# A graph layer's product copied by VectorE, and one eviction of the attention layer moved ahead of a norm in ScalarE's order

## The chip, the cores and the metric

The kernel runs on one core of one Trainium2 chip. A core has five engines with instruction streams of their own: TensorE (PE, with its weight loads shown apart as PEld), VectorE (DVE), ScalarE (ACT), GpSimd (POOL) and SyncE (SP), which in this kernel issues all DMA transfers. [...]The metric is the device time of the program in microseconds, lower is better: the median of several runs.

## The reference

The input is 64 images `x` of 256 rows by 512 columns in fp32, and one 256 x 256 graph `adj` that all of them share. Two layers follow each other, each with a residual and a layer norm over the columns:

```
mi = x @ Wi.T;  mj = x @ Wj.T
x  = layernorm(x + deg * (mi + b) + a @ mj)          # a = adj as float, deg = its row sums
q, k, v = x @ Wq.T + bq, x @ Wk.T + bk, x @ Wv.T + bv    # 8 heads of 64 columns
s  = where(adj == 0, -inf, q @ k.T / 8);  o = softmax(s) @ v
x  = layernorm(x + o @ Wo.T + bo)
```

Everything is computed in fp32. A matmul of fp32 operands appears as two PE instructions in the trace.

## The kernel before

**Tiling.** An image is held as two tiles of 128 rows. Images are worked on in pairs; pair g is `b1 = 2g` and `b2 = 2g + 1`. The main loop runs 31 times. Pass g holds the attention of pair g and, woven into it, layer 0 of pair g+1, and at its end the q, k and v products of pair g+1. One pass lasts about 96 us.

**Products in seven steps.** Products of a 2 x 2 block matrix with a 2 x 2 block weight are done by the scheme of Strassen and Winograd: seven products of blocks and some sums (`S1` to `S4` on the left, `T1` to `T4` on the right, the latter made once). Each step function issues one product on PE and then the instructions that take its bank of PSUM away. Several products share a bank: they are added up in it, and such a later product has to wait until the earlier content has been read. There are three banks of this kind (`ps_m`, tag `mm`).

**Layer 0** (`l0_steps`) has step1 to step7. Step4 (bank y) is read by VectorE (line 542). Step5 makes bank z from `S1` and `T1` and copies it to `mj[:, 1]` (line 547). Step6 adds into bank y and is read by VectorE as `u3` (line 551); POOL adds `u3` to `mj[:, 1]` (line 552), and `split` cuts the sum into two parts, `hi` on ScalarE (line 524) and `lo` on POOL (line 525). Step7 adds into bank z, and so needs step5's copy to be done; it is read at line 561. `neighbours` multiplies the graph by `hi` and `lo`. `take` forms the residual and the norm's statistics of a row tile, whose last part, `rstd`, is made on POOL (line 461). `give` applies the norm on ScalarE (lines 466 and 467: `shift`, then the row tile). `send_h` stores a row tile of the result in DRAM, and with the second tile starts a load that brings the image back in another layout as `hB` (line 603). VectorE transposes `hB` into `hT` (line 485), which feeds the q, k and v products. `sum_x` makes the four sums `xS` of the next image with lines 477 to 480 of VectorE.

**q, k, v and the output.** `qkv_steps` makes the seven steps of one of the three, `o_steps` those of the output product. `second_late` puts the third step ahead of the second. For q and k the first step is evicted by ScalarE with the bias (line 711, two instructions, `u`); the next one in the list adds into the same bank, and so needs that eviction to be done. Each step takes its weight block from a ring of nine buffers and starts the load of a later block into the buffer that became free (line 442).

**Attention.** `scores` multiplies q by k for two heads into a pair of banks (`ps`; two such pairs); VectorE adds the mask (line 805), ScalarE takes exponentials (line 809), POOL adds halves of them (`pk`, line 812). `values` multiplies by v, `divide` sums the denominators on PE (`den`), inverts them on VectorE (line 882) and spreads them by DMA. `neighbours` uses one of the score pairs too.

**Order.** The lists handed to `run` are written out by hand and set the order in which instructions are recorded. Instructions recorded through `in_order` keep that order on their engine; the framework's scheduler places the others by their operands. In the pass's tail the order is `o[0], neighbours, take1, take0, q[0], give1, send1, o[1], give0, send0, multiply`, the sums of the output product, then `k[0], q[1], k[1]`. On each engine instructions then run strictly in order.

Of the kernel before, what the change touches and what calls it, by code (L numbers as in the profile page):

```python
# [224 lines left out]
def unshifted_path(ctx, tc, flag, x, adj, wiT, wjT, b0, wqT, bq, wkT, bk, wvT, bv, woT, bo, out):  # L225
# [16 lines left out]
    nc = tc.nc  # L242
# [26 lines left out]
    def bank(name):  # L269
        return ps_m.tile([P, 512], F32, tag="mm", name=name)  # L270

    def score_banks(name):
        return ps_s.tile([P, 2, 512], F32, tag="sc", name=name)
# [8 lines left out]
    def in_order(ins):  # L282

        tc.keep_in_program_order(ins)
# [4 lines left out]
    def matmul(*args, **kw):  # L289
        in_order(nc.tensor.matmul(*args, **kw))  # L290
# [7 lines left out]
    def load_x(b):  # L298
        if b < B:
            xh[b] = p6.tile([P, NT, D], F32, tag="xh", name="xh")  # L300
            nc.sync.dma_start(out=xh[b], in_=x[b].rearrange("(t p) d -> p t d", p=P))
# [22 lines left out]
    xT, xS, hT, hS, qT, kT, vv, aoT, oS = ({} for _ in range(9))  # L324
# [48 lines left out]
    def add_bias(b):  # L373
        in_order(nc.gpsimd.tensor_tensor(xh[b], xh[b], degb, ALU.add))
# [76 lines left out]
    def norm_stats(t, order=anywhere):  # L451
        st = small.tile([P, 6], F32, tag="st", name="st")
        order(nc.vector.bn_stats(st, t))
        mv = small.tile([P, 2], F32, tag="mv", name="mv")
        nc.vector.bn_aggr(mv, st)
        ve = small.tile([P, 1], F32, tag="ve", name="ve")
        nc.vector.tensor_scalar(ve, mv[:, 1:2], EPS, None, ALU.add)
        below = small.tile([P, 1], F32, tag="below", name="below")
        order(nc.vector.tensor_scalar(below, mv[:, 0:1], -1.0, None, ALU.mult))  # L459
        rstd = small.tile([P, 1], F32, tag="rstd", name="rstd")  # L460
        nc.gpsimd.tensor_tensor(rstd, ve, mhalf, ALU.pow)  # L461
        return below, rstd

    def norm_apply(t, below, rstd, order=anywhere):
        shift = small.tile([P, 1], F32, tag="shift", name="shift")
        order(nc.scalar.activation(shift, below, AF.Identity, scale=rstd))  # L466
        order(nc.scalar.activation(t, t, AF.Identity, bias=shift, scale=rstd))  # L467
# [8 lines left out]
    def left_steps(f, order=anywhere):  # L476
        return [lambda: order(nc.vector.tensor_add(f["S1"], f["A21"], f["A22"])),
                lambda: order(nc.vector.tensor_sub(f["S2"], f["S1"], f["A11"])),
                lambda: order(nc.vector.tensor_sub(f["S3"], f["A11"], f["A21"])),
                lambda: order(nc.vector.tensor_sub(f["S4"], f["A12"], f["S2"]))]  # L480
# [21 lines left out]
    def l0_steps(b):  # L502
        banks, k = {}, {}

        def product(name, left, n, first):
            if first:
                banks[name] = bank("po")
            for c in range(2):
                matmul(banks[name], left[:, c, :], w0[:, n, c, :], start=(first and c == 0),
                                 stop=(c == 1), skip_group_check=True)  # L510

        def raw(t, h):
            return xT[b][:, 2 * h:2 * h + 2, t * P:(t + 1) * P]

        def keeper(name):
            k[name] = p3.tile([P, D], F32, tag="lu", name=name)
            return k[name]

        def add_scaled(t, src):
            nc.vector.scalar_tensor_tensor(xh[b][:, t, :], src, deg[:, t:t + 1], xh[b][:, t, :],  # L520
                                           ALU.mult, ALU.add)

        def split(t):
            nc.scalar.copy(k["hi"][:, t, :], k["mj"][:, t, :])
            nc.gpsimd.tensor_tensor(k["lo"][:, t, :], k["mj"][:, t, :], k["hi"][:, t, :].bitcast(F32),
                                    ALU.subtract)

        def step1():
            product("x", raw(0, 0), B11, True)
            nc.scalar.copy(keeper("u1"), banks["x"])  # L530

        def step2():
            product("w", raw(1, 1), T4, True)
            add_scaled(1, banks["w"])

        def step3():
            product("x", raw(0, 1), B21, False)
            add_scaled(0, banks["x"])

        def step4():  # L540
            product("y", xS[b]["S2"], T2, True)
            nc.vector.tensor_add(keeper("u2"), banks["y"], k["u1"])

        def step5():
            product("z", xS[b]["S1"], T1, True)
            k["mj"] = p1.tile([P, NT, D], F32, tag="mj", name="mj")
            nc.scalar.copy(k["mj"][:, 1, :], banks["z"])  # L547

        def step6():
            product("y", xS[b]["S3"], T3, False)  # L550
            nc.vector.tensor_add(keeper("u3"), banks["y"], k["u1"])
            nc.gpsimd.tensor_tensor(k["mj"][:, 1, :], k["mj"][:, 1, :], k["u3"], ALU.add)

            k["hi"] = p1.tile([P, NT, D], F32R, tag="hi", name="hi")
            k["lo"] = p1.tile([P, NT, D], F32R, tag="lo", name="lo")
            split(1)
            add_scaled(1, k["u3"])

        def step7():
            product("z", xS[b]["S4"], B22, False)  # L560
            nc.vector.tensor_add(k["mj"][:, 0, :], banks["z"], k["u2"])
            split(0)

        stats = {}

        def neighbours():
            k["pa"] = score_banks("pa")
            for i in (1, 0):
                for n, (j, part) in enumerate((j, part) for j in (1, 0) for part in ("hi", "lo")):
                    matmul(k["pa"][:, i, :], graph[:, j, i * P:(i + 1) * P], k[part][:, j, :],  # L570
                           start=(n == 0), stop=(n == 2 * NT - 1))

        def take(t):
            r = xh[b][:, t, :]
            in_order(nc.vector.tensor_add(r, k["pa"][:, t, :], r))
            stats[t] = norm_stats(r, in_order)

        def give(t):
            norm_apply(xh[b][:, t, :], *stats[t], in_order)


        return [step1, step2, step3, step4, step5, step6, step7, neighbours, lambda: take(1), lambda: take(0),
                lambda: give(1), lambda: send_h(b, 1), lambda: give(0), lambda: send_h(b, 0)]

# [83 lines left out]
    def second_late(steps):  # L668
        return [steps[0], steps[2], steps[1], *steps[3:]]
# [239 lines left out]
    def run(steps):  # L909
        for s in steps:  # L910
            s()
# [4 lines left out]
    def order_of(name):  # L916
        return [(name, n) for n in RIGHT]

    for g in range(-1, NG - 1):
        o, q, k, v = (order_of(name) for name in ("wo", "wq", "wk", "wv"))  # L920
# [18 lines left out]
    p, q = l0_steps(0), l0_steps(1)  # L939
# [18 lines left out]
    o = second_late(qk_steps(0, qT, "qT", bq_sb, bqd, True))  # L958
    k = second_late(qk_steps(0, kT, "kT", bk_sb, bkd, True))
# [22 lines left out]
    for g in range(NG - 1):  # L982
        load_x(NB * (g + 2))
        load_x(NB * (g + 2) + 1)
        work = layer0(g + 1)
        run(work[0])
        for w in range(2, NB * NC, 2):
            values(g, w - 2)
            values(g, w - 1)
            multiply()  # L990
            divide_two(g, w - 1)
            scores(g, w)()
            if w == 4:
                run(work[2])
            later = scores(g, w + 1)
            later()
            run(work[w // 2 if w < 4 else w // 2 + 1])
        w = NB * NC - 2
        values(g, w)
        values(g, w + 1)  # L1000
        multiply()
        o = o_steps(g)
        q = second_late(qk_steps(g + 1, qT, "qT", bq_sb, bqd))
        k = second_late(qk_steps(g + 1, kT, "kT", bk_sb, bkd, True))
        v = second_late(v_steps(g + 1, True))
        neighbours, take1, take0, give1, send1, give0, send0 = work[SLOTS + 1]
        divide_two(g, w + 1)
        run([o[0], neighbours, take1, take0, q[0], give1, send1, o[1], give0, send0, multiply,
             *left_steps(oS[g], in_order), k[0], q[1], k[1]])
        run(o[2:6] + work[SLOTS + 2] + [v[0], o[6], v[1]])  # L1010
        end = finish_steps(g)
        k = with_output_bias(g + 1, k)[2:]
        run(q[2:5] + end[:1] + q[5:6] + end[1:2] + q[6:7] + end[2:3] + k[:1] + end[3:4] + k[1:] + end[4:] + v[2:3])
        turn_x(NB * (g + 2))
        sum_x(NB * (g + 2))
        if g + 2 < NG:
            add_bias(NB * (g + 2))
        run(v[3:5])
        run([scores(g + 1, 0), scores(g + 1, 1)])
        run(v[5:])  # L1020
# [3 lines left out]
    g = NG - 1  # L1024
# [89 lines left out]
```

## Time and profile before

| | |
|---|---|
| time, median of 3 runs | 3117.08 us (3116.3 to 3118.02) |
| profiled execution, its own time | 3115.82 us |
| its span | 3113.4 us |
| granted TensorE clock | 0.999 |
| PE busy with matmuls | 3071.3 us, 99% |
| VectorE busy | 2148.5 us, 69% |
| POOL busy | 1520.8 us, 49% |
| ScalarE busy | 1007.8 us, 32% |
| DMA queue of SP | 48.3% of 16 engines' span |
| copy of `mj` on ScalarE (L547) | 64 times, 575 ns each |
| eviction of k's first step (L711, `u<-st,bk`) | 64 instructions, 458 ns each |

Times are those of one execution on the chip. A row of a timeline has the start in us from the span's start, the duration, the engine, the line, the operation, what is written and read, the shape, and in brackets how long the engine had been idle and what ended that. Rows of the same kind that follow each other are merged (x8: eight of them, with their common duration). A row of the waits has the waiting engine and line, what it waited for, the sum in us, the number of times and the longest one. A chain that ended last is given on the page too, but it covers nothing of the main loop here, so it is not used.

### The profile page before, as it was taken

To read this page: it belongs to the slowest core of one execution; us is meant where nothing else is said; L and a number is where in the kernel's file an instruction comes from. 1 tells how busy PE (TensorE), PEld (TensorE's weight loads), DVE (VectorE), ACT (ScalarE), POOL (GpSimd) and SP (SyncE) were. 2 spreads that over 40 slices of the span, in tenths; PEclk is the share of its full clock that TensorE was granted. 3 is DMA by queue.
4 is the path that set the end of the run, shared out by engine and by line. 5 is a ranking of instruction groups with operands and counts; after the bars stand their busy time and mean duration, and the time that the engine had idled before them with its cause. 6 is when DMAs were issued, how large, how long until landed. Compare 5 with 4: busy or idle time off the path is not lost. (4 is left out here: it accounts for less than half of the span.)

```text
span 3113.4 us, 42777 instructions
## 1 busy us (share of the span) xinstructions
PE 3071.3 (99%) x14598; PEld 2117.8 (68%) x14598; DVE 2148.5 (69%) x3234; ACT 1007.8 (32%) x1925; POOL 1520.8 (49%) x1255
## 2 busy tenths in 40 slices
PE   7999999999999999999999999999999999999998
PEld 5667766677766677666776667766677766677665
DVE  6776676766777667676667676667766667767665
ACT  2333333323333333333233332333333333323332
POOL 2544445544545445454454554454544546445453
PEclk9999999999999999999999999999999999999999
DMA  7345544455444555445553445544455444555333
GB/s 256 121 143 156 166 124 134 128 157 165 141 124 123 157 166 152 117 131 149 157 166 118 131 134 157 165 139 123 127 155 169 146 118 127 154 162 160 116 111 98
DMA packets 410395, 447.28 MB, mean 144 GB/s; under 512 B 40896, under 2 KB 300224, under 8 KB 409792
## 3 DMA queue, kind: packets, MB, share of 16 engines
q1 hardware_dynamic: 410176, 444.50, 48.3%
q8 instruction: 120, 1.97, 0.3%
q14 instruction: 99, 0.81, 0.1%
HBM read 340.79 MB, written 70.25 MB: 132 GB/s over the span
## 5 line engine op out<-in xcount | busy, mean ns | idle before, releaser
L461 POOL TENSOR_TENSOR rstd<-ve,mhalf 128x1 f32<-128x1 f32 x256 | 140.6, 554 | 724.3 <-DVE below L459 724.3
L812 POOL TENSOR_TENSOR pk<-pe 128x512 f32<-128x512 f32 x256 | 322.3, 1275 | 341.0 <-ACT pe L809 341.0
L290 PE MATMUL po<-w,xS 128*128 128x512 f32 x1024 | 470.4, 602 | 6.1 <-ACT mj L547 5.6
L290 PE MATMUL st<-hS,factor 128*128 128x256 f32 x2048 | 452.7, 379 | 1.2 <-DVE u L685 1.2
L290 PEld LDWEIGHTS st<-hS,factor 128*128 128x128 f32 x2048 | 388.4, 190 | 55.1 <-DVE u L685 1.6
L809 ACT ACTIVATE pe<-pe 128x1024 f32<-128x1024 f32 x256 | 270.8, 1058 | 379.2 <-DVE pe L805 379.2
L290 PE MATMUL st<-hT,factor 128*128 128x256 f32 x1536 | 360.7, 381 | 9.0 <-ACT u L711 8.4
L290 PE MATMUL po<-w,xT 128*128 128x512 f32 x768 | 352.3, 601 | 13.8 <-DVE xT L485 11.3
L290 PEld LDWEIGHTS po<-w,xS 128*128 128x128 f32 x1024 | 186.8, 190 | 252.2 <-issue 191.5
L290 PEld LDWEIGHTS st<-hT,factor 128*128 128x128 f32 x1536 | 289.0, 190 | 61.5 <-ACT u L711 20.8
L805 DVE TENSOR_TENSOR pe<-ps,maskT 128x1024 f32<-128x1024 f32 x256 | 297.8, 1194 | 35.3 <-PE ps L290 35.3
L882 DVE RECIPROCAL rden<-den 128x256 f32<-128x256 f32 x127 | 222.8, 1754 | 73.7 <-PE den L290 68.2
L290 PEld LDWEIGHTS po<-w,xT 128*128 128x128 f32 x768 | 143.9, 191 | 181.4 <-issue 163.0
L290 PE MATMUL ps<-qT,kT 64*128 64x256 f32 x2048 | 264.9, 392 | 0.0
L883 POOL TENSOR_TENSOR rtot<-rtot,rden 128x256 f32<-128x256 f32 x127 | 92.8, 730 | 330.2 <-DVE rden L882 330.2
L290 PE MATMUL pav<-pe,v_sb 128*64 128x256 f32 x2048 | 250.1, 386 | 1.9 <-ACT pe L809 1.8
L740 DVE TENSOR_TENSOR xh<-st,xh 128x512 f32<-128x512 f32 x186 | 144.5, 777 | 149.7 <-PE st L290 149.7
L290 PEld LDWEIGHTS pav<-pe,v_sb 128*64 128x64 f32 x2048 | 135.2, 136 | 154.2 <-issue 72.0
L290 PEld LDWEIGHTS ps<-qT,kT 64*128 64x128 f32 x2048 | 184.3, 186 | 78.2 <-issue 51.3
L290 PE MATMUL st<-factor,hS 128*128 128x256 f32 x1024 | 234.8, 382 | 0.0
L290 PE MATMUL st<-factor,oS 128*128 128x256 f32 x992 | 224.2, 379 | 0.0
L290 PEld LDWEIGHTS st<-factor,hS 128*128 128x128 f32 x1024 | 191.9, 190 | 35.4 <-issue 10.6
(115 smaller groups left out, 4657.0 us busy)
## 6 DMA issues: line engine op xcount, KB each, us to landing
xB<-in_x_dram SPq DMA_DIRECT2D x256, 128.0 KB, 3.9
xh<-in_x_dram SPq DMA_DIRECT2D x64, 512.0 KB, 4.4
factor<-wq SPq DMA_DIRECT2D x128, 256.0 KB, 4.4
factor<-wk SPq DMA_DIRECT2D x128, 256.0 KB, 2.7
factor<-wv SPq DMA_DIRECT2D x128, 256.0 KB, 2.7
spread<-rden SPq DMA_DIRECT2D x1016, 32.0 KB, 1.9
factor<-wo SPq DMA_DIRECT2D x124, 256.0 KB, 3.3
h_cols<-xh SPq DMA_DIRECT2D x124, 256.0 KB, 2.5
```

Of the source, the lines that this page charges most:

```text
L290: in_order(nc.tensor.matmul(*args, **kw))
L461: nc.gpsimd.tensor_tensor(rstd, ve, mhalf, ALU.pow)
L740: nc.vector.tensor_add(dst, src, dst)
L805: nc.vector.tensor_add(pe.rearrange("p j t q -> p j (t q)"), ps.rearrange("p j t q -> p j (t q)"), maskT.rearrange("p t q -> p (t q)").uns ...
L809: in_order(nc.scalar.activation(flat, flat, AF.Exp, scale=QSCALE, accum_out=etot[:, NB * g + i, pr:pr + 1]))
L812: nc.gpsimd.tensor_tensor(pk, pe[:, :, 0, :], pe[:, :, 1, :], ALU.add)
L882: nc.vector.reciprocal(rden, den)
L883: nc.gpsimd.tensor_tensor(rtot, rtot, rden, ALU.add)
```

## The change

Two edits. In step5 of layer 0 the copy of bank z into `mj[:, 1]` is given to VectorE instead of ScalarE. In the tail of a pass, `k[0]` (the first product of k and its eviction) is recorded right after `o[1]`, ahead of `give0` and `send0`, and no longer after the sums of the output product. PE's order stays what it was, and so does POOL's. On ScalarE the two eviction instructions of k now stand ahead of the second row tile's `shift` and norm. On SP's queue the store of the second row tile of h now stands behind two more loads of weight blocks, and the load of `hB` behind one load that followed it before. On VectorE the copy stands behind the two mask sums (image b1), or behind line 542 (image b2), and ahead of line 551.

```diff
@@ l0_steps @@
         def step5():
             product("z", xS[b]["S1"], T1, True)
             k["mj"] = p1.tile([P, NT, D], F32, tag="mj", name="mj")
-            nc.scalar.copy(k["mj"][:, 1, :], banks["z"])
+            nc.vector.tensor_copy(k["mj"][:, 1, :], banks["z"])
@@ unshifted_path, tail of a pass @@
-        run([o[0], neighbours, take1, take0, q[0], give1, send1, o[1], give0, send0, multiply,
-             *left_steps(oS[g], in_order), k[0], q[1], k[1]])
+        run([o[0], neighbours, take1, take0, q[0], give1, send1, o[1], k[0], give0, send0, multiply,
+             *left_steps(oS[g], in_order), q[1], k[1]])
```

## The prediction

> **What bounds the kernel now.** I read the page first, then the list of waits, then the timeline of one pass of the main loop (31 passes, one for each pair of images). The page:
>
> ```profile
> span 3113.4 us, 42777 instructions
> ...
> PE 3071.3 (99%) x14598; PEld 2117.8 (68%) x14598; DVE 2148.5 (69%) x3234; ACT 1007.8 (32%) x1925; POOL 1520.8 (49%) x1255
> ```
>
> PE has work at all times and every other engine has room. So time is won only where PE itself stands. The list of waits names what PE stands for; two entries occur 31 times, once a pass, and both name ScalarE:
>
> ```profile
> PEld po L290 <- ACT mj L547: 31.3, 31, 1.0
> ...
> PEld st L290 <- ACT u L711: 20.8, 31, 0.7
> ```
>
> They are weight loads and partly overlap matmuls, so the price is taken from starts on PE. First wait, in the pass from 1056 to 1152 us:
>
> ```profile
> 1067.13 3.70 PE L290 MATMUL po<-w,xS 128*128 128x512 f32 x8
> ...
> 1069.34 1.06 ACT L809 ACTIVATE pe<-pe 128x1024 f32<-128x1024 f32 x1
> ...
> 1070.39 0.56 ACT L547 COPY mj<-po 128x512 f32<-128x512 f32 x1
> ...
> 1071.01 1.98 PE L290 MATMUL po<-w,xS 128*128 128x512 f32 x4 [0.18 <-ACT mj L547]
> ...
> 1089.28 7.13 PE L290 MATMUL po<-w,xS 128*128 128x512 f32 x16
> ```
>
> Step 5's product ends near 1069.1, but its copy stands behind two exponentials on ScalarE and ends at 1070.95. Step 7, which adds into the same bank, starts at 1071.01. Image b2's four such products (16 matmuls) run unbroken from 1089.28 to the next row's start at 1096.34: 7.06 us. Image b1's sixteen, with the wait, run from 1067.13 to 1074.64: 7.51. The wait with its restart costs 0.45 us.
>
> Second wait:
>
> ```profile
> 1105.94 3.62 PE L290 MATMUL st<-hT,factor 128*128 128x256 f32 x16
> ...
> 1107.91 0.28 ACT L466 ACTIVATE shift<-below,rstd 128x1 f32<-128x1 f32 x1
> ...
> 1108.94 0.82 ACT L711 ACTIVATE u<-st,bk 128x256 f32<-128x256 f32 x2
> ...
> 1109.81 1.99 PE L290 MATMUL st<-hT,factor 128*128 128x256 f32 x8 [0.26 <-ACT u L711]
> ```
>
> k's first product is done by 1107.83, yet its eviction waits until the second norm row (shift, then 0.81 us of apply) is through. k's next product, for the same bank, starts only at 1109.81. Three products take 1105.94 to 1111.64, 5.70 us; one unbroken takes 1.73 (1104.21 to 1105.94), three 5.18. Cost: 0.52 us.
>
> **What the Trainium skill says.** "SBUF — State Buffer", section "Who interferes with whom": a VectorE instruction with two SBUF inputs and a GpSimd instruction that reads SBUF exclude each other, the later one to issue blocks fully, and VectorE with at most one SBUF input does not contend. The trace agrees: L479 takes 1.50 us while `lo` runs on POOL and 0.42 elsewhere; L551, with one PSUM input, takes 0.69 in the middle of a POOL sum of 1.26. "VectorE: DVE Perf Modes", section "Why PSUM operands drop a tier": an fp32 operand in PSUM keeps VectorE at one element per cycle. The 0.69 of L551 fits it. "Perfetto Trace Analysis", section "Identifying the Most-Contended Engine": matmul busy share does not measure distance from the peak; here it reads 99% while about 1 us a pass is lost, which agrees.
>
> **Part 1: the copy on VectorE.** It takes away 64 copies of 0.58 us on ScalarE and adds 64 on VectorE. No row shows this form; the nearest are the PSUM cast of 256 columns, 0.41, and the PSUM sum of 512 columns, 0.69. I estimate 0.68. In VectorE's order it stands behind the two mask sums (end 1069.30) and before L551, which waits for PE until 1070.87; VectorE is idle for 1.56 us there, so the copy is hidden, ends near 1069.95, and frees the bank 0.7 us before step 7's turn at 1070.67. For b2 it falls into an idle time of 2.68 us and ends near 1093.65, with PE asking at 1094.5. Without this cover each copy would put 0.68 us ahead of L551. PE gains 0.45 at step 7, if nothing else holds it later. That needs looking at:
>
> ```profile
> 1071.90 1.71 POOL L552 TENSOR_TENSOR mj<-mj,u 128x512 f32<-128x512 f32 x1
> ...
> 1073.03 0.69 DVE L561 TENSOR_TENSOR mj<-po,u 128x512 f32<-128x512 f32 x1 [0.55 <-PE po L290]
> ...
> 1074.34 2.73 POOL L525 TENSOR_TENSOR lo<-mj,hi 128x512 fp32r<-128x512 f32 x2 [0.73 <-ACT hi L524]
> ...
> 1074.43 1.50 DVE L479 TENSOR_TENSOR xS<-xT 128x256 f32<-128x256 f32 x1
> 1075.86 1.50 DVE L480 TENSOR_TENSOR xS<-xT,xS 128x256 f32<-128x256 f32 x1
> 1077.28 1.75 DVE L882 RECIPROCAL rden<-den 128x256 f32<-128x256 f32 x1
> 1078.94 1.16 DVE L805 TENSOR_TENSOR pe<-ps,maskT 128x1024 f32<-128x1024 f32 x1
> ```
>
> PE's next scores start at 1080.21 and need the bank that L805 has read at 1080.10: 0.11 us of slack. L805 stands behind L882, and that behind L480, which POOL's two `lo` hold up. POOL's chain (pk, L552, `lo`) does not hang on step 7. If it stays, L805 stays, and PE gives back all but some 0.06 us (0.11 less the 0.05 from release to start).
>
> But L561 moves up by 0.45, to 1072.58, and L477 behind it to 1073.19, where L552 still has the port. A blocked two-input instruction ends 0.28 us behind POOL's (1075.93 against 1075.65, 1077.35 against 1077.07). So L477 ends at 1073.61 + 0.28 = 1073.89, and L479, which follows L477's end by 0.38 in every pass, starts at 1074.27. `lo` starts 0.73 behind L552, at 1074.34. Today L479 comes 0.09 too late; then it comes 0.07 early. From L478 (0.25 before `lo`, 256 elements at 0.96 GHz = 0.267, `lo` delayed by 0.04) I estimate VectorE's lead-in as 0.03 longer than POOL's: 0.04 us remains in L479's favour. Then `lo` waits 0.22, L480 ends near 1076.1, and L882 waits only for PE's `den`, now 0.45 earlier; L805 ends near 1079.6 and PE goes on at 1079.76. I take this: 0.45. `lo` itself ends at 1077.25, 1.2 us before PE wants it.
>
> **Part 2: k's product earlier.** PE's and POOL's orders are unchanged. k's eviction goes to 1107.91 to 1108.73, ahead of k's next product (1109.4); gain 0.52. The second apply moves from 1109.03 to 1109.85 at its end; q's eviction behind it waits for PE until 1109.55 anyway and ends where it did. Late next is the second half of h. On SP's queue its store now stands behind two factor loads more, of which the later waits for PE's 1109.55: issue 1109.06 becomes about 1110.1, landing about 1.3 later; one later factor load passes ahead of the hB load, and factors have microseconds in hand. hB landed 1.5 to 3.3 us before VectorE's transpose in these passes (median 2.3). Less 1.3, less the 0.52 by which PE is now early, some 0.5 remains, and PE has 0.23 more at the first S product. In the tightest passes that is short: 0 to 3 us in the whole run, I take 1.5.
>
> **Prologue.** VectorE gets two copies, but in image 0's second norm L457 now goes ahead of a 0.69 us subtraction: about 0.5 us gained where PE waits for that row (45.03).
>
> **Sum.** 31 x (0.45 + 0.52) = 30.1, + 0.5 - 1.5 = 29.1 us. The profiled execution took 3115.82 us (span 3113.4 and 2.4 around it): 3086.7. The median of the runs shown is 1.26 above it: 3088.
>
> **Rivals.**
> 1. POOL's `lo` wins the port, or L477 doesn't move: part 1 keeps 0.06 a pass, 31 x 0.58 + 0.5 - 1 = 17.5: 3099.6. For it: a margin of 0.04 us out of an inferred lead-in. Against: where VectorE's L520 starts 0.11 ahead of L552 it wins, in all 31 passes.
> 2. The copy takes the shared port after all: the first pk, due 0.2 after it, slips by up to 0.45, POOL's chain with it, and PE stands at 1080.21 and 0.4 longer: 31 x 0.12 = 4 us gained, 3113, no change that shows. Against: L551.
> 3. Slower: hB late. Place: VectorE's transpose of the second image, then PE's S products. About 0.7 us a pass is free after the change; each further microsecond costs 31. At 1.7 later than worked out the gain is gone; at 2.7 later, 3148. For it: hB's landing varies between 3.2 and 5.8. Against: a long landing went with a short store before it, so issue of the store to landing of hB varies only by 1.7.
>
> **Chances.** Both parts 0.62 (own range 3085 to 3091), rival 1 0.20, something between or beyond 0.06, rival 2 0.06, rival 3 0.06. A change under 0.2%, 6.2 us, can hardly be told from none here. Faster 0.88, same 0.06, slower 0.06. Range 3084 to 3101, which holds the first two.
>
> **What would show it.** Both ScalarE entries gone from PE's waits. b1's sixteen products in 7.06 us. L479 near 0.42 and the first `lo` near 1.5 us if VectorE has the port; L479 still 1.50 and PE waiting for L805 if not. Three k and q products in 5.2 us. Wrong would be: PE or VectorE waiting for hB in most passes, or pk above 1.3 us.

## The result, and the profile after

| | before | after |
|---|---|---|
| time, median of four runs each | 3116.69 us (3115.23 to 3118.02) | 3114.93 us (3113.84 to 3116.38) |
| profiled execution, its own time | 3115.82 us | 3116.38 us |
| its span | 3113.4 us | 3114.5 us |
| ratio after to before, 95% interval | | 0.9995 (0.9977 to 1.0012) |

No difference can be measured. The forecast was 3088, with a range of 3084 to 3101: wrong by 27 us. The page of the kernel after:

```profile
span 3114.5 us, 42683 instructions
...
PE 3066.7 (98%) x14598; PEld 2125.4 (68%) x14598; DVE 2200.1 (71%) x3298; ACT 967.4 (31%) x1861; POOL 1505.3 (48%) x1255
```

The number of instructions in the first line has fallen by 94, though the change only moves work from one engine to another. 63 of these are the semaphore instructions shown further down. VectorE has 51.6 us more to do (64 copies at 0.68 are 43.5), ScalarE 40.4 less.

**Both forecast gains are there.** The timeline of the kernel after, at the same place as the one shown of before (image b1, then the products of k and q; start, duration, engine, line, operation, in brackets the idle time ahead of it and what ended it):

```profile
1067.54 5.42 PE L290 MATMUL po<-w,xS 128*128 128x512 f32 x12
...
1069.63 0.68 DVE L547 COPY mj<-po 128x512 f32<-128x512 f32 x1
...
1073.61 0.70 DVE L477 TENSOR_TENSOR xS<-xT 128x256 f32<-128x256 f32 x1
...
1074.61 1.95 PE L290 MATMUL pav<-pe,v_sb 128*64 128x256 f32 x16
1074.69 0.42 DVE L479 TENSOR_TENSOR xS<-xT 128x256 f32<-128x256 f32 x1
1074.76 2.90 POOL L525 TENSOR_TENSOR lo<-mj,hi 128x512 fp32r<-128x512 f32 x2 [0.73 <-ACT hi L524]
1075.02 1.50 DVE L480 TENSOR_TENSOR xS<-xT,xS 128x256 f32<-128x256 f32 x1
...
1077.19 1.76 DVE L882 RECIPROCAL rden<-den 128x256 f32<-128x256 f32 x1 [0.67 <-PE den L290]
...
1106.67 5.34 PE L290 MATMUL st<-hT,factor 128*128 128x256 f32 x24
...
1108.96 0.82 ACT L711 ACTIVATE u<-st,bk 128x256 f32<-128x256 f32 x2
...
1111.85 1.46 PE L290 MATMUL st<-factor,aoT 128*128 128x256 f32 x6
```

The sixteen products of b1 run from 1067.54 to 1074.61: 7.07 us, where before had 7.51. The copy takes 0.68. L479 starts 0.07 ahead of `lo` and takes 0.42, so VectorE has the read port; L882 waits for PE's `den` and nothing else. The three products of k and q run from 1106.67 to 1111.85: 5.18 us, where before had 5.70. No wait for ScalarE's L547 or L711 occurs 31 times any more.

**Two new waits have taken their place.** From the list of waits of the kernel after (waiting engine and line, what it waited for: sum in us, times, longest):

```profile
PEld pa L290 <- POOL lo L525: 29.3, 31, 1.0
...
PE pa L290 <- POOL lo L525: 15.9, 31, 0.5
...
DVE hT L485 <- DMA hB<-h_cols: 5.5, 6, 1.8
```

The first two are one event: PE's product of the graph and the second `lo` of image b2 stands for POOL, once a pass. The third is `hB`, late in six passes. (A weight load of `den` that waits for `lo`, 11.9 us in 31 times, is new in the list too. It stands with the same figures in e3, e5 and e6 below, which lose nothing by it.)

**What made `lo` late.** First the kernel before, timeline around b2's sixth product, a stretch that the prediction did not show:

```profile
1094.73 0.69 DVE L551 TENSOR_TENSOR u<-po,u 128x512 f32<-128x512 f32 x1 [2.68 <-PE po L290]
1095.46 0.75 DVE L520 SCALAR_TENSOR_TENSOR xh<-u,deg,xh 128x512 f32<-128x512 f32 x1
1095.57 1.80 POOL L552 TENSOR_TENSOR mj<-mj,u 128x512 f32<-128x512 f32 x1 [1.48 <-DVE u L551]
1096.13 2.16 DVE L485 STREAM_TRANSPOSE hT<-hB 128x1024 f32<-128x1024 f32 x1
...
1098.13 0.70 DVE L561 TENSOR_TENSOR mj<-po,u 128x512 f32<-128x512 f32 x1
...
1099.57 1.27 POOL L525 TENSOR_TENSOR lo<-mj,hi 128x512 fp32r<-128x512 f32 x1 [0.18 <-ACT hi L524]
```

Then the kernel after, the same instructions:

```profile
1094.70 0.69 DVE L551 TENSOR_TENSOR u<-po,u 128x512 f32<-128x512 f32 x1 [1.02 <-PE po L290]
1095.43 1.85 DVE L520 SCALAR_TENSOR_TENSOR xh<-u,deg,xh 128x512 f32<-128x512 f32 x1
1095.47 1.26 POOL L552 TENSOR_TENSOR mj<-mj,u 128x512 f32<-128x512 f32 x1 [1.42 <-DVE u L551]
...
1097.20 2.13 DVE L485 STREAM_TRANSPOSE hT<-hB 128x1024 f32<-128x1024 f32 x1
...
1099.24 0.64 DVE L561 TENSOR_TENSOR mj<-po,u 128x512 f32<-128x512 f32 x1
...
1100.61 1.28 POOL L525 TENSOR_TENSOR lo<-mj,hi 128x512 fp32r<-128x512 f32 x1 [1.85 <-ACT hi L524]
...
1101.94 0.50 PE L290 MATMUL pa<-lo,graph 128*128 128x512 f32 x1 [0.49 <-POOL lo L525]
```

L520 (the residual, two SBUF inputs) and L552 (POOL's sum) both start when L551 is done and want the same read port. Before, L520 starts 0.11 us ahead and runs unhindered (0.75) while L552 is held (1.80). After, its lead is 0.04, L552 runs unhindered (1.26) and L520 is held (1.85; it ends at 1097.28, 0.55 behind POOL). The transpose and L561 stand behind L520 and end 1.1 us later, L561 feeds the second `hi`, that the second `lo`, and PE stands for it. L520 starts as long behind L551 as it did; it is L552 that starts earlier: its median distance from L551's end fell from 0.144 to 0.079 us (before, one of the 31 passes has 0.442).

The reason shows in the instructions recorded under L552. Before (engine, operation, number, ns, first and last start):

```profile
L552 POOLq EVENT_SEMAPHORE  x64: 17/17/43, 23.3 to 3015.1; - x64
```

After:

```profile
L552 POOLq EVENT_SEMAPHORE  x1: 17/17/17, 46.8 to 46.8; - x1
```

L552 reads `u3`, made by VectorE, and `mj[:, 1]`, copied by ScalarE before and by VectorE after. With producers on two engines there was a separate semaphore instruction on POOL's queue ahead of L552. "Perfetto Trace Analysis" of the Trainium skill, section "Identifying Dependency Chains", says that an instruction waiting on several engines may get such instructions put in front of it; this trace agrees. With both on VectorE one wait is left, the extra instruction is gone, and POOL is 0.065 us quicker to the port. In b1 the same instruction is gone and nothing moves: POOL is still busy with `pk` when L551 ends, and L552 starts 0.335 us behind L551's end before and after.

**The balance.** For each kernel, the distance between the starts of fixed PE instructions of a pass, less the same distance in the kernel before, mean of 30 passes, us (columns e1 to e7 are the experiments below):

| place on PE | after | e1 | e2 | e3 | e4 | e5 | e6 | e7 |
|---|---|---|---|---|---|---|---|---|
| step 7 of b1 | -0.45 | -0.45 | 0 | -0.45 | 0 | -0.45 | -0.45 | -0.45 |
| second `lo` product of b2 | +0.78 | +0.78 | 0 | 0 | +0.78 | 0 | 0 | 0 |
| k's second product | -0.54 | +0.31 | -0.54 | -0.54 | +0.31 | -0.54 | -0.54 | -0.54 |
| first S product (`hB` late) | +0.18 | 0 | +0.13 | +0.07 | 0 | +0.08 | +0.05 | +0.08 |
| sum | -0.03 | +0.63 | -0.39 | -0.91 | +1.08 | -0.91 | -0.93 | -0.91 |
| times 31 | -1.0 | +19.7 | -12.2 | -28.3 | +33.4 | -28.1 | -28.7 | -28.1 |
| median less that of before | -1.8 | +20.6 | -11.9 | -27.6 | +35.1 | -26.3 | -29.2 | -26.7 |

The last two rows differ by 1.8 us at most, so four places account for the time of all eight kernels. (The sums and their multiples are of unrounded values.)

### The profile page after: what moved, and what is told of

Read it like the earlier page. It is cut to its first block, busy times and chain, and to the rows that moved or that the text cites. A ratio compares the mean times of both kernels' runs of the same rounds, so it can differ in the third digit from the quotient of the medians.

```text
span 3114.5 us, 42683 instructions
## 1 busy us (share of the span) xinstructions
PE 3066.7 (98%) x14598; PEld 2125.4 (68%) x14598; DVE 2200.1 (71%) x3298; ACT 967.4 (31%) x1861; POOL 1505.3 (48%) x1255
## 5 line engine op out<-in xcount | busy, mean ns | idle before, releaser
L290 PE MATMUL po<-w,xS 128*128 128x512 f32 x1024 | 462.4, 599 | 0.4 <-DVE xS L478 0.4
L290 PE MATMUL st<-hT,factor 128*128 128x256 f32 x1536 | 352.6, 380 | 0.7 <-ACT hT L622 0.7
L805 DVE TENSOR_TENSOR pe<-ps,maskT 128x1024 f32<-128x1024 f32 x256 | 298.1, 1195 | 35.3 <-PE ps L290 35.3
L882 DVE RECIPROCAL rden<-den 128x256 f32<-128x256 f32 x127 | 223.1, 1757 | 92.2 <-PE den L290 89.0
L525 POOL TENSOR_TENSOR lo<-mj,hi 128x512 fp32r<-128x512 f32 x128 | 175.2, 1378 | 107.3 <-ACT hi L524 107.3
```

The lines of the kernel that those rows point to most:

```text
L805: nc.vector.tensor_add(pe.rearrange("p j t q -> p j (t q)"), ps.rearrange("p j t q -> p j (t q)"), maskT.rearrange("p t q -> p (t q)").uns ...
L882: nc.vector.reciprocal(rden, den)
```

## The experiments

In the expectations P is the theory above: POOL takes the port in b2. K: moving k's product makes `lo` late. V: VectorE has simply too much to do in b2. H: `hB` is late because of its store's place in SP's order. e1 to e4 are timed against 3116.31 us of the kernel before, e5 to e7 against 3116.34.

**e1: the copy alone.** The kernel before, with

```diff
-            nc.scalar.copy(k["mj"][:, 1, :], banks["z"])
+            nc.vector.tensor_copy(k["mj"][:, 1, :], banks["z"])
```

> Both images' copies of bank z by VectorE, k's product in its old place. Theory P (the read port, lost in image b2): PE's 0.45 us at step 7 of b1 goes, and 0.78 us at the second lo product of b2 comes, 0.33 a pass, +10 us against before: about 3127. Rival K (it is k's move that makes lo late): no wait for lo here, 31 x 0.45 = 14 us gained: about 3103.

3136.94 us, ratio 1.0063 (1.0046 to 1.0080). The first half of the change alone makes the kernel slower. From its waits:

```profile
PEld st L290 <- ACT u L711: 30.4, 31, 1.0
PEld pa L290 <- POOL lo L525: 29.3, 31, 1.0
```

The wait for `lo` is there without the move of k: K falls. It came out 10 us above what P gave, because the wait for k's eviction, 20.8 us in the kernel before, has grown to 30.4. The late neighbours make b2's second norm late, and k's eviction still stands behind that norm: +0.31 a pass. With k moved ahead of the norm the same lateness costs PE nothing there, as the column of the full change shows. The two edits are not additive: 20.6 and -11.9 (e2) make 8.7, and both together gave -1.8; of the difference, 10.5, this 0.31 us makes 9.6.

**e2: k's move alone.** The kernel before, with

```diff
-        run([o[0], neighbours, take1, take0, q[0], give1, send1, o[1], give0, send0, multiply,
-             *left_steps(oS[g], in_order), k[0], q[1], k[1]])
+        run([o[0], neighbours, take1, take0, q[0], give1, send1, o[1], k[0], give0, send0, multiply,
+             *left_steps(oS[g], in_order), q[1], k[1]])
```

> k's product in its new place, both copies by ScalarE as before. Theory P: PE's 0.54 us a pass at k's second product goes, no wait for lo, and hB lands late in some passes as in the changed kernel (0.18 us a pass on average): -0.36 a pass, about 3106. Rival K: PE waits 0.78 us for lo here too, +0.4 a pass: about 3130.

3104.40 us, ratio 0.9957 (0.9940 to 0.9974), as P gave it. The wait for the copy remains, that for `lo` is absent, and `hB` is late in seven instances:

```profile
PEld po L290 <- ACT mj L547: 31.3, 31, 1.0
...
DVE hT L485 <- DMA hB<-h_cols: 3.6, 7, 0.9
```

So the late `hB` belongs to k's move and `lo` to the copy.

**e3: b1's copy on VectorE, b2's on ScalarE.** The changed kernel, with

```diff
-            nc.vector.tensor_copy(k["mj"][:, 1, :], banks["z"])
+            (nc.scalar.copy if b % NB else nc.vector.tensor_copy)(k["mj"][:, 1, :], banks["z"])
```

> As the changed kernel, but the copy of image b2 stays with ScalarE, where it had 0.9 us to spare. Theory P: L552 of b2 waits for two engines again, L520 starts 0.11 us ahead of it and has the port, no wait for lo: -0.99 + 0.18 a pass, about 3092. Rival V (VectorE is too full in b2's stretch): also about 3092. Rival K: lo is still late, about 3115.

3088.67 us, ratio 0.9910 (0.9893 to 0.9926). Nearly the whole forecast gain (27.6 of 29.1 us) is back by undoing one copy of two, the one of the image in which nothing waited for it.

**e4: b2's copy alone.** The kernel before, with

```diff
-            nc.scalar.copy(k["mj"][:, 1, :], banks["z"])
+            (nc.vector.tensor_copy if b % NB else nc.scalar.copy)(k["mj"][:, 1, :], banks["z"])
```

> Only the copy of image b2 by VectorE, all else as before. Theories P and V: the wait for lo by itself, +0.78 a pass, about 3141, and L520 of b2 takes 1.85 us. Rival K: nothing late, about 3117.

3151.37 us, ratio 1.0107 (1.0090 to 1.0124): slower by 35.1 us, the 0.78 and the 0.31 of the table; the 0.31 was again not in P's figure. From its waits, all three:

```profile
PEld po L290 <- ACT mj L547: 31.3, 31, 1.0
...
PEld pa L290 <- POOL lo L525: 29.3, 31, 1.0
...
PE st L290 <- ACT u L711: 17.9, 31, 0.6
```

e3 and e4 place the loss in b2's copy, but do not tell P from V. The next two do.

**e5: the second wait put back.** The changed kernel; in b2 VectorE copies 511 of the 512 columns and ScalarE the last one, so that L552 again has two engines to wait for:

```diff
-            nc.vector.tensor_copy(k["mj"][:, 1, :], banks["z"])
+            nc.vector.tensor_copy(k["mj"][:, 1, :D - b % NB], banks["z"][:, :D - b % NB])
+            if b % NB: nc.scalar.copy(k["mj"][:, 1, D - 1:], banks["z"][:, D - 1:])
```

> As the changed kernel, but of image b2's copy VectorE takes 511 columns and ScalarE the last one, so that L552 waits for both engines again while VectorE's work is the same. Theory P: L552 starts some 0.06 us later behind L551, L520 has the port again (0.75 us, not 1.85), the wait for lo is gone: -0.99 + 0.18 a pass, about 3092. Rival V (VectorE's added work makes lo late): no change against the changed kernel, about 3115.

3090.07 us, ratio 0.9915 (0.9899 to 0.9932). VectorE has as much to do as in the changed kernel, and the loss is gone: V falls. Instructions under L552 in e5:

```profile
L552 POOLq EVENT_SEMAPHORE  x32: 17/17/43, 48.1 to 2990.1; - x32
```

And its timeline around b2's sixth product:

```profile
1088.36 0.69 DVE L551 TENSOR_TENSOR u<-po,u 128x512 f32<-128x512 f32 x1 [1.03 <-PE po L290]
1089.08 0.75 DVE L520 SCALAR_TENSOR_TENSOR xh<-u,deg,xh 128x512 f32<-128x512 f32 x1
1089.19 1.79 POOL L552 TENSOR_TENSOR mj<-mj,u 128x512 f32<-128x512 f32 x1 [1.48 <-DVE u L551]
1089.75 2.18 DVE L485 STREAM_TRANSPOSE hT<-hB 128x1024 f32<-128x1024 f32 x1
```

The semaphore instruction is back for b2's images, L520 leads by 0.11 again and has the port, and the transpose follows at once. VectorE is idle for only 1.03 us ahead of L551, as in the changed kernel: the copy was and is hidden.

**e6: the residual out of POOL's way.** The changed kernel; in b2 L520 is recorded behind L561:

```diff
@@ step6 @@
-            add_scaled(1, k["u3"])
+            if b % NB == 0: add_scaled(1, k["u3"])
@@ step7, behind split(0) @@
+            if b % NB: add_scaled(1, k["u3"])
```

> As the changed kernel, but image b2's L520 stands behind L561 in VectorE's order, where nothing but the reciprocal waits behind it. Theory P: L552 may start as early as it likes, L485 and L561 no longer wait behind a blocked L520: the wait for lo is gone, about 3092. Rival V: about 3115.

3087.11 us, ratio 0.9908 (0.9891 to 0.9924). Its timeline at the same place:

```profile
1085.90 2.13 DVE L485 STREAM_TRANSPOSE hT<-hB 128x1024 f32<-128x1024 f32 x1
1086.06 1.29 POOL L552 TENSOR_TENSOR mj<-mj,u 128x512 f32<-128x512 f32 x1 [1.42 <-DVE u L551]
...
1087.93 0.65 DVE L561 TENSOR_TENSOR mj<-po,u 128x512 f32<-128x512 f32 x1
1088.08 2.95 POOL L525 TENSOR_TENSOR lo<-mj,hi 128x512 fp32r<-128x512 f32 x2 [0.73 <-ACT hi L524]
1088.51 1.40 DVE L520 SCALAR_TENSOR_TENSOR xh<-u,deg,xh 128x512 f32<-128x512 f32 x1
```

POOL keeps the port for L552 and nothing that PE needs stands behind it. L520 is now held by `lo` instead (1.40), where no one on PE's path waits for it. Both copies stay on VectorE.

**e7: the store of h from ScalarE's queue.** e3, with

```diff
-        nc.sync.dma_start(out=h_cols[b]...
+        (nc.scalar if (i, t) == (1, 0) else nc.sync).dma_start(out=h_cols[b]...
```

> As e3, and the store of b2's second half of h is issued by ScalarE's queue, not behind two factor loads on SP's. Theory H (hB late by its place in SP's order costs 0.18 us a pass): the wait for hB is gone, 5 us less than e3, about 3086. Rival (hB's landing is set by the DMA engines, not by the issue): as e3, 3092. If ScalarE's queue stalls on the transfer's own wait, slower than e3.

3089.65 us, ratio 0.9915 (0.9898 to 0.9931). The store of the second half was issued 0.37 us earlier than in e3 (mean 0.41 against 0.78 behind the start of k's second product), but landed only 0.10 earlier (5.65 against 5.75). The transpose's wait for `hB`, in e7:

```profile
  DMA hB<-h_cols: 2.2, 4
```

and in e3:

```profile
  DMA hB<-h_cols: 1.8, 4
```

The wait for `hB` stays and the time is that of e3, so H is not borne out. But the test is a weak one, as it could undo only a part of the delay: measured from the start of k's second product, the store is issued at -0.73 us in the kernel before, at 0.78 in e3 and at 0.41 in e7. SP's order makes 0.37 of these 1.51 us. The rest comes with the move itself: k's product starts 0.54 us earlier, and the second norm, which the store has to wait for, now stands behind k's eviction.

The store by itself takes longer, 3.8 us on average from issue to landing in the kernel before, 4.9 after, 5.0 in e3 and 5.2 in e7. The load of `hB` behind it takes less in return, 4.6 us before, 3.8 after, 3.6 in e3 and 3.7 in e7. From the store's issue to the landing of `hB` that makes 8.4, 8.7, 8.7 and 9.0. So `hB` comes later mainly because its store is issued later. Why the store takes longer and the load less is open.

**Faster than both.** e3, e5 and e6 all beat the kernel before by some 26 to 29 us; the slowest of their runs took 3092.84 us, the fastest of the changed kernel 3113.84. Their ranges overlap, so they are not ranked (e6 3086.18 to 3089.31, e3 3087.69 to 3089.72, e5 3088.20 to 3092.84).

## Why the prediction was wrong

**What held.** The 0.45 us of part 1 measured 0.449 a pass. The chain of events for it came as forecast: the copy hidden, L477 and L479 pulled forward, L479 0.07 ahead of `lo` and in possession of the port, L805 out of the way. The 0.52 of part 2 measured 0.537. The estimate of 0.68 for the copy was right (0.687 on average). Rival 1, the port lost in b1, did not happen; nor did rival 2.

**What held by luck, or was read too well.** That L479 would keep the port rested on an inferred difference of 0.03 us between the lead-ins of VectorE and POOL (the time from a recorded start to the reading). It came from L478, which won 0.25 us ahead of `lo`, and some 0.27 us for reading its 256 columns: sums of 256 columns take 0.42 here, of 512 columns 0.69. By that figure L520 with its lead of 0.044 should have won as well, and it lost every time. So the outcome in b1 was right, but the margin of 0.04 us behind it is not confirmed. "Two entries occur 31 times" is true of PE's matmul rows alone (`PE st <- ACT u` 8.4 us, `PE po <- ACT mj` 5.6); among the weight loads that the prediction quoted, other waits come as often, such as `PEld pav <- DVE xS L478`, 23.5 us in 31 times. The prices were taken from starts on PE, so they do not suffer. L551's 0.69 says nothing of PSUM, as VectorE's sums of two SBUF tensors of that size (L477 of `hS`) take 0.69 too. And 99% busy leaves room for the 1 us lost in 96; e3 shows more, where the span fell by 27.6 us and PE's busy time (3071.3 to 3054.8) by 16.5 only.

**The step that failed** is in part 1: "For b2 it falls into an idle time of 2.68 us and ends near 1093.65, with PE asking at 1094.5." The copy did fall into idle time (2.68 became 1.02), and as a piece of VectorE's work it cost nothing. But this step looked only at the engine that receives the copy. It did not ask who reads the copy's result, and how that reader's waits change when the producer changes its engine. L552 lost a wait, started 0.065 us earlier and took the port. Rival 1 even quoted the lead concerned, "where VectorE's L520 starts 0.11 ahead of L552 it wins, in all 31 passes", as support for b1's case, and took it as a fixed property of that place. It was a race with 0.11 us between the two, and the change moved one of its runners. The cost, which the prediction put at nothing, was +0.776 us a pass, 24.1 us in all, of an error of 27.

**A mis-sized term.** The late `hB` was priced at 0 to 3 us in the run, 1.5 taken; it came to 31 x 0.182 = 5.6. The place and the mechanism (a few passes, VectorE's transpose, then PE's S products) were right. Part of the excess follows from the step that failed: in the changed kernel the late `lo` delays the second norm too, and the store is issued 1.07 us behind the start of k's second product, against 0.78 in e3. Where `lo` is in time, e3, e5, e6 and e7 lose 1.6 to 2.5 us by `hB`, inside the range, and e2 4.2. Each of these is read from one execution, and the landings vary by more than a microsecond from pass to pass, so not all of the difference need come from the store's issue. The prologue's 0.5 gain is not shown: over the first 65 us the eight kernels differ by -0.15 to +2.7 us from the kernel before without a pattern.

With the measured terms the prediction's sum reads 31 x (-0.449 - 0.537 + 0.776 + 0.182) = -0.9 us, against -1.8 in the medians.

Rival 3 had the right sign of the danger (hB late) but not its size; no rival had b2's port.

## What to carry to other kernels

When an operation changes its engine, look at the readers of its result as well as at the two engines: a reader that waited for two engines and now waits for one starts earlier, and if it shares a port with something else, a race that had one outcome in every pass can have the other in every pass. Before calling a move free, list the pairs of VectorE and POOL instructions that start close to each other (0.11 us here), with what stands behind each. An instruction that nothing on PE's path waits for (L520 here) belongs behind those that feed this path.

## What the runs showed of the hardware

- **Who gets the read port is decided within tens of nanoseconds.** "SBUF — State Buffer" of the Trainium skill, section "Who interferes with whom", says that the order of issue decides who blocks. That one of the two is held agrees with these traces, but the one with the earlier recorded start is not always the one that gets the port: L520 recorded 0.044 us ahead of L552 (mean; after, e1, e4) lost in all 31 passes, 0.108 ahead or more (before, e2, e3, e5, e7) it won in all 31, and L479, a plain sum of two tensors, 0.070 ahead of `lo` won. The point at which L520 begins to win lies between 0.044 and 0.108 and was not measured closer. Whether issue differs from the recorded start by so much, or something else decides such near ties, no run here shows.
- **A second engine to wait for cost POOL about 0.065 us where POOL stood idle** (L552 of b2): one more instruction of 17 ns on its queue, and a start 0.144 instead of 0.079 us behind the last producer's end. In b1, where POOL was busy, it cost nothing.
- **A wait cost PE more than the list of waits shows.** The wait for `lo` has 15.9 us in PE's row, 0.51 a pass, and PE lost 0.776 by its starts. Of these 0.670 is the later start of the product that waited and 0.106 the later start of the one behind it: that product takes 0.50 us and its neighbours 0.40. The two waits that the change removed show the same second part, 0.104 us each.
